# One array for all eight PSUM banks, in a planner-ordered two-layer transformer kernel on one core

## The chip, the core and the metric

The kernel runs on one core of a Trainium2 chip. It is one launch. The metric is the device time of that launch in microseconds: the median of three runs of the kernel before is 1513.48 us (1513.02 to 1515.63). The engines are TensorE (PE, with its weight loads as PEld), VectorE (DVE), ScalarE (ACT), GpSimd (POOL) and SyncE (SP), which issues most transfers.

## The reference

Two transformer layers on x of 2048 rows by 256 columns, all in 32 bits. Each layer adds to x the normed output of an attention block, and then the normed output of a gated FFN. Cut to what matters:

```python
x = x + _layernorm(_L0_attn_ref(_layernorm(x), ...))   # latent q and kv, rotary, 16 heads of 16, causal
x = x + _layernorm(_L0_ffn_ref(_layernorm(x), ...))    # silu(x wg * sg) * (x wu * su), then wdown * sd; int8 weights
x = x + _layernorm(_L1_attn_ref(_layernorm(x), ...))   # plain qkv, 16 heads of 16, causal
x = x + _layernorm(_L1_ffn_ref(_layernorm(x), ...))
# attention: softmax(q k^T * scale + causal mask) v, then the output projection
```

## The kernel before, in words

**Units.** The 2048 rows are cut into four chunks of 512 (CH), and each chunk into four tiles of 128. Sixteen heads are taken in four groups of four (NG). One *unit* is a chunk c of queries with a group g of heads: 16 units a layer, in the order (0,0), (0,1), then all groups of chunks 1, 2 and 3, then (0,2), (0,3) (L780). Each unit has two parts.

**Maxima** (L611 to 697). The largest score of each query row is found first, so that the softmax can subtract it. For each of two head pairs i and each half e of PE's rows, a *fill* (L628 to 631) multiplies a query tile with 512 keys into one PSUM bank named m, and a DVE reduce (L656) takes its row maxima. Fills use 64 of PE's 128 rows: e = 0 the upper half, e = 1 the lower, and the two halves can work side by side. A unit has 8c fills for each pair beside the diagonal ones: `diagonal` (L636) fills two banks with the mask and the scores, `block` b and c fill what lies under the diagonal. `close` (L675) joins the maxima, PE transposes them (mt, L692), and ACT copies them into mrow (L696).

**Weighted sum** (L699 to 763). For each key tile kt and each pair i, PE writes the score pair s: two banks side by side, first minus the maximum (a selector times mrow, L716), then K times Q added to it (L721). ACT takes the exp of both banks in one instruction (L726, 1024 columns), POOL zeroes what lies above the diagonal (L730), and PE adds V times the result into the bank av (L737), which stays in use for the whole unit. At the unit's end ACT copies av out (L745), PE transposes it (ot, L750) and DVE divides (L757, L759).

**Projections and FFN.** `proj0`, `proj1` and `qkv_heads` make Q, K and V of a chunk; Q and K go to DRAM and come back stacked (L460 to 475). `mixed` (L765) is the output projection. `ffn` (L803) runs per chunk eight steps of gate and up (a pair of banks gu, L868), then silu on ACT (L875), the product on DVE (L877), a high part on ACT (L879) and the low rest on POOL (L880), and the down products dn (L835), which add up in two banks over eight steps.

**What sets the order.** The kernel hands every piece of work to a `Plan` (L96) as an operation with an engine, an estimated time, its buffers and a rank (its due time in units). `Plan.run` (L122) sets the order of each engine's queue before the program exists: it repeats a choice of the operation that can start first by its own clock, and among those of that engine within NEAR (0.3 us) of it the one of the lowest rank. An operation can start when those it depends on have ended plus HOP, when its buffers are free plus HOP, and when its engine (on PE: its row half) is free; a change of PE's mode (row halves, column groups, full) adds SWITCH. `lag` is added after an operation's end for those that depend on it. The engines then run their queues in order, and waits are put between them where a buffer is read, written or used again. The fills of unit n have ranks from n - 1.4 on, the scores of unit n from n on, so that the maxima of the next unit stand beside the weighted sum of this one.

**PSUM before.** There are eight banks of 512 columns. They are bound to three pools (L198 to 200): `ps` has two pairs (s and gu), `ps_m` three single banks, all under the tag m (fills, transposes, projections, dn, fz, mt, ot, wo), `ps_av` one bank (av). Each is a ring: its places are given in turn, and the next one may be taken when all that used it have been put in the order.

```python
ps = ctx.enter_context(tc.tile_pool(name="ps", bufs=2, space=PSUM))       # pairs: s, gu
ps_m = ctx.enter_context(tc.tile_pool(name="ps_m", bufs=3, space=PSUM))   # single banks: m
ps_av = ctx.enter_context(tc.tile_pool(name="ps_av", bufs=1, space=PSUM)) # av
```

Of the kernel before, what the change touches and what calls it, by code (L numbers as in the profile page):

```python
# [11 lines left out]
F32 = mybir.dt.float32  # L12
# [51 lines left out]
class Buf:  # L64


    def __init__(self, make, ring=None):
        self.make, self.ring = make, ring
        self.tile = None
        self.users, self.writers, self.readers = [], [], []  # L70
        if ring is not None:
            ring.asked.append(self)
# [15 lines left out]

class Op:
# [6 lines left out]
class Plan:  # L96
# [3 lines left out]
    HOP, NEAR, SWITCH = 0.15, 0.3, 0.25  # L100
# [21 lines left out]
    def run(self):  # L122
# [9 lines left out]
        while ready:  # L132
            best = []
            for o in ready:
                at = max((d.end + self.HOP for d in o.after), default=0.0)
                wanted = {}
                for b in o.bufs:
                    if b.ring is not None and b.tile is None:
                        ring = b.ring
                        n = wanted.get(ring, 0)  # L140
                        wanted[ring] = n + 1
                        if ring.ordered and ring.asked[ring.given + n] is not b:
                            at = None
                            break
                        old = ring.slots[(ring.at + n) % len(ring.slots)]
                        if old is not None:
                            if any(u.end is None for u in old.users):
                                at = None
                                break
                            at = max(at, max(u.end for u in old.users) + self.HOP)  # L150
# [13 lines left out]
            for b in o.bufs:  # L164
                if b.ring is not None and b.tile is None:
                    b.ring.slots[b.ring.at] = b
                    b.ring.at = (b.ring.at + 1) % len(b.ring.slots)
                    b.ring.given += 1
                b.t
# [19 lines left out]
def kernel(ctx: ExitStack, tc: tile.TileContext, x_in, cols_in, rows_in, wd_in, wuq_in, rot_in,  # L189
# [8 lines left out]
    ps = ctx.enter_context(tc.tile_pool(name="ps", bufs=2, space=PSUM))  # L198
    ps_m = ctx.enter_context(tc.tile_pool(name="ps_m", bufs=3, space=PSUM))
    ps_av = ctx.enter_context(tc.tile_pool(name="ps_av", bufs=1, space=PSUM))  # L200


    rings = {}

    def new(pool, shape, dtype, tag, name, n):

        ring = rings.setdefault(tag, Ring(n, tag not in ("m", "s")))
# [3 lines left out]
    def bank(name):  # L211
        return new(ps_m, [P, CH], F32, "m", name, 3)
# [6 lines left out]

    def psum2(name):  # L220
        return ps.tile([P, 2, CH], F32, tag="s", name=name)

    def psum1(name):
        return ps_m.tile([P, CH], F32, tag="m", name=name)
# [375 lines left out]
    def attention(layer, plan, wo, wob, bo, scale):  # L600
        L, KS, Vs, kb, vb = layer.L, layer.K, layer.V, layer.kb, layer.vb
        with tc.tile_pool(name=f"kv{L}", bufs=1) as kv, tc.tile_pool(name=f"at{L}", bufs=1) as at:
# [8 lines left out]
            def maxima(n, c, g, qb):  # L611
# [10 lines left out]
                def block(name, i, e, terms, us, reduces, red_us, kc, dst):  # L622
# [10 lines left out]
                    plan.op("PE", us, fill, r=[qb, kb[kc][g]], w=[s], hold=[dst], rank=rk, mode="row", lanes=(e,), lag=0.3)  # L633
                    plan.op("DVE", red_us, lambda: reduces(s.t), r=[s], w=[dst], rank=rk)

                def diagonal(i):  # L636
# [14 lines left out]
                    plan.op("PE", 1.2, fill, r=[qb, kb[c][g], mask_b, mx_b], w=ss, hold=[pm], rank=rk, mode="row", lag=0.3)  # L651
                    for e in range(2):
                        plan.op("DVE", 0.63, lambda e=e: top(pm.t[:, :, e, i, 1], tiles(ss[e].t)), r=[ss[e]], w=[pm], rank=rank())
# [7 lines left out]
                for i in range(2):  # L661
                    diagonal(i)
                    for e in range(2):
                        block("b", i, e, [(3, 0, 3 * P, 0), (1, 0, P, 3 * P)], 0.4,
                              lambda s, i=i, e=e: top(pml.t[:, e, i, 0:4], tiles(s)), 0.63, c, pml)
# [3 lines left out]
                    for t in range(TPC):  # L669
                        for p in range(c):  # L670
                            for e in range(2):
                                block(f"{t}{p}", i, e, [(t, 0, CH, 0)], 0.22,
                                      lambda s, i=i, e=e, t=t, p=p: top(pm.t[:, t, e, i, 2 + p:3 + p], s), 0.63, p, pm)
# [25 lines left out]
            def weighted(n, c, g, qb, mrow):  # L699
                av = Buf(lambda: ps_av.tile([P, CH], F32, tag="av", name=f"av{L}{n}"), rav)  # L700
# [3 lines left out]
                for kt in range(last + 1):  # L704
# [3 lines left out]
                    for i in range(2):  # L708
                        s = new(ps, [P, 2, CH], F32, "s", f"s{L}{n}{kt}{i}", 2)
# [3 lines left out]
                        def score(s=s, kt=kt, i=i, off=off, nq=nq):  # L713
# [5 lines left out]
                            for e in range(2):  # L719
# [5 lines left out]
                                mode="row", lag=0.3)  # L725
# [52 lines left out]
            rav = Ring(1)  # L778
# [24 lines left out]
    def ffn(L, sg_at, su_at, after=()):  # L803

        with tc.tile_pool(name=f"fw{L}", bufs=1) as fw, tc.tile_pool(name=f"ff{L}", bufs=1) as ff:
# [54 lines left out]
            for n_, c in enumerate(order):  # L860
                halves = []
                for fc in range(8):
                    rk = 10 * n_ + fc
                    s = new(ps, [P, 2, CH], F32, "s", f"gu{L}{c}{fc}", 2)
# [189 lines left out]
```

## Time and profile before

| what | before |
|---|---|
| median of 3 runs | 1513.48 us (1513.02 to 1515.63) |
| the profiled execution's own time | 1515.71 us |
| its span, first to last instruction | 1513.8 us |
| mean granted TensorE clock | 0.934 |
| ACT exp, L726, 640 instructions | 546.3 us busy |
| PE score pair, L716 and L721, 2560 instructions | 331.5 and 298.8 us busy |
| PE av, L737, 2560 instructions | 303.0 us busy |
| HBM read and written | 41.66 and 35.65 MB |

The two attention layers lie at about 60 to 655 us and 800 to 1366 us, the FFNs at 655 to 780 us and from 1366 us to the end. One ot (L750) stands at each unit's end; in the first layer those of chunk 3 are at 502.5, 548.5, 589.7 and 625.0 us.

How to read it: the page gives each engine's busy time, its share of the span, and the costliest groups of instructions with the idle time before them and what ended it. PE's matmuls are pipelined and their ends are modelled, so that PE can be called busy while its next matmul waits. PEld is the load of the weights of a matmul and shows waits that PE itself hides. The waits view sums who waited for whom: total, times, the longest. The windows view gives each engine's busy time in a stretch of the span, the granted clock and the transfers.

### The profile page before, as it was taken

To read this page: it belongs to the slowest core of one execution; us is meant where nothing else is said; L and a number is where in the kernel's file an instruction comes from. 1 tells how busy PE (TensorE), PEld (TensorE's weight loads), DVE (VectorE), ACT (ScalarE), POOL (GpSimd) and SP (SyncE) were. 2 spreads that over 40 slices of the span, in tenths; PEclk is the share of its full clock that TensorE was granted. 3 is DMA by queue.
4 is the path that set the end of the run, shared out by engine and by line. 5 is a ranking of instruction groups with operands and counts; after the bars stand their busy time and mean duration, and the time that the engine had idled before them with its cause. 6 is when DMAs were issued, how large, how long until landed. Compare 5 with 4: busy or idle time off the path is not lost. (4 is left out here: it accounts for less than half of the span.)

```text
span 1513.8 us, 22232 instructions
## 1 busy us (share of the span) xinstructions
PE 1352.8 (89%) x8632; PEld 767.1 (51%) x8632; DVE 936.8 (62%) x1932; ACT 798.5 (53%) x1094; POOL 289.5 (19%) x468
## 2 busy tenths in 40 slices
PE   2468999999999999869878999999999999986986
PEld 2234455555555454436745555555555454444764
DVE  1266578859897883335434668886898888234432
ACT  1232555555556667646443255555655676754553
POOL 2011101110001000235523010110000100033543
PEclk9686999999999999979978699999999999988998
DMA  4532040022000000020045222004000000000000
GB/s 145 183 128 93 27 168 15 15 88 108 15 15 1 15 15 15 1 70 1 1 167 204 72 74 84 15 15 174 22 15 15 15 1 15 15 1 1 15 15 28
DMA packets 42617, 78.74 MB, mean 52 GB/s; under 512 B 3891, under 2 KB 8336, under 8 KB 42384
## 3 DMA queue, kind: packets, MB, share of 16 engines
q1 hardware_dynamic: 42080, 75.85, 14.4%
q8 instruction: 68, 1.11, 0.3%
q0 software_dynamic: 144, 1.16, 0.2%
q10 hardware_dynamic: 288, 0.31, 0.1%
q14 instruction: 37, 0.30, 0.1%
HBM read 41.66 MB, written 35.65 MB: 51 GB/s over the span
## 5 line engine op out<-in xcount | busy, mean ns | idle before, releaser
L726 ACT ACTIVATE pt<-s 128x1024 f32<-128x1024 f32 (+3 forms) x640 | 546.3, 895 | 350.6 <-PE s L721 343.2
L656 DVE TENSOR_REDUCE pm<-m 128x1 f32<-128x512 f32 x768 | 476.2, 682 | 55.3 <-PE m L630 49.9
L716 PE MATMUL s<-mrow,sel 64*128 64x512 f32 (+3 forms) x1280 | 331.5, 405 | 6.9 <-ACT mrow L696 4.6
L737 PE MATMUL av<-pt,V 128*32 128x512 f32 (+3 forms) x2560 | 303.0, 548 | 2.9 <-POOL pt L730 2.9
L721 PE MATMUL s<-Q,K 64*128 64x512 f32 (+3 forms) x1280 | 298.8, 367 | 0.0
L630 PE MATMUL m<-K,Q 64*128 64x512 f32 x768 | 284.7, 489 | 9.1 <-DVE pm L656 0.4
L730 POOL TENSOR_SCALAR_AFFINE_SELECT pt<-pt 128x256 f32<-128x256 f32 x256 | 103.0, 407 | 832.5 <-ACT pt L726 830.5
L716 PEld LDWEIGHTS s<-mrow,sel 64*128 64x128 f32 x1280 | 174.1, 189 | 86.6 <-ACT pt L726 54.4
L630 PEld LDWEIGHTS m<-K,Q 64*128 64x128 f32 x768 | 119.5, 188 | 181.8 <-DVE pm L656 150.5
L721 PEld LDWEIGHTS s<-Q,K 64*128 64x128 f32 x1280 | 188.8, 190 | 11.9
L877 DVE SCALAR_TENSOR_TENSOR fu<-gu,cols,sl 128x512 f32<-128x512 f32 x64 | 47.6, 747 | 88.0 <-ACT sl L875 88.0
L880 POOL TENSOR_TENSOR fl<-fu,fh 128x512 fp32r<-128x512 f32 x64 | 82.1, 1287 | 99.7 <-ACT fh L879 99.7
L737 PEld LDWEIGHTS av<-pt,V 128*32 128x32 f32 x2560 | 52.3, 109 | 87.6 <-issue 72.2
L868 PE MATMUL gu<-fx,wg 128*128 128x512 f32 x256 | 77.2, 424 | 10.5 <-DVE fu L877 4.2
L868 PE MATMUL gu<-fx,wu 128*128 128x512 f32 x256 | 72.5, 407 | 0.0
L875 ACT ACTIVATE sl<-gu,cols 128x512 f32<-128x512 f32 x64 | 43.7, 687 | 39.9 <-PE gu L868 39.6
L868 PEld LDWEIGHTS gu<-fx,wg 128*128 128x128 f32 x256 | 49.3, 201 | 27.6 <-DVE fu L877 9.2
L879 ACT CAST fh<-fu 128x512 fp32r<-128x512 f32 x64 | 39.5, 621 | 36.8 <-DVE fu L877 36.8
L835 PE MATMUL dn<-fh,wdn 128*128 128x512 f32 x128 | 52.9, 413 | 3.6 <-ACT yn_f L402 2.3
L868 PEld LDWEIGHTS gu<-fx,wu 128*128 128x128 f32 x256 | 50.5, 198 | 11.2 <-issue 0.5
L835 PE MATMUL dn<-fl,wdn 128*128 128x512 f32 x128 | 52.3, 409 | 0.3
L428 PE MATMUL tr_f<-ident,xn_f 128*128 128x128 f32 x64 | 16.0, 335 | 28.2 <-ACT xn_f L402 25.5
(763 smaller groups left out, 1449.9 us busy)
## 6 DMA issues: line engine op xcount, KB each, us to landing
K<-sc_k SPq DMA_DIRECT2D x32, 512.0 KB
Q<-sc_q SPq DMA_DIRECT2D x32, 512.0 KB
sc_k<-kh SPq DMA_DIRECT2D x32, 256.0 KB
sc_k<-kl SPq DMA_DIRECT2D x32, 256.0 KB
sc_q<-qh SPq DMA_DIRECT2D x32, 256.0 KB
sc_q<-ql SPq DMA_DIRECT2D x32, 256.0 KB
x<-in_x_dram SPq DMA_DIRECT2D x4, 512.0 KB
out_dram<-x SPq DMA_DIRECT2D x4, 512.0 KB
```

Of the source, the lines that this page charges most:

```text
L630: nc.tensor.matmul(s.t[:, to:to + k1 - k0], qb.t[b:b + 64, i, t * P:(t + 1) * P], KS[kc][b:b + 64, 2 * g + i, k0:k1], start=True, stop=True)
L656: nc.vector.tensor_reduce(dst, src, AX.X, ALU.max)
L716: nc.tensor.matmul(s.t[:, e, 0:nq], sel[b:b + 64, i, :], mrow.t[b:b + 64, off:CH], start=True, stop=False)
L721: nc.tensor.matmul(s.t[:, e, 0:nq], KS[kt // TPC][b:b + 64, 2 * g + i, k * P:(k + 1) * P], qb.t[b:b + 64, i, off:CH], start=False, stop=True)
L726: plan.op("ACT", 0.19 + nq / 620, lambda s=s, pt=pt, nq=nq: nc.scalar.activation(pt.t[:, :, 0:nq], s.t[:, :, 0:nq], AF.Exp, scale=scale), ...
L730: plan.op("POOL", 0.41, lambda pt=pt: nc.gpsimd.affine_select(out=pt.t[:, :, 0:P], in_=pt.t[:, :, 0:P], compare_op=ALU.is_ge, fill=0.0, ba ...
L737: nc.tensor.matmul(av.t[32 * j:32 * j + 32, off:CH], Vs[kt // TPC][:, kt % TPC, DV * h:DV * h + 32], pts[kt, j // 2].t[:, j % 2, 0:nq], st ...
L835: nc.tensor.matmul(dn[dh].t, wdn[:, fc, dh * P:(dh + 1) * P], halves[fc][j].t, start=fc == 0 and j == 0, stop=fc == 7 and j == 1)
L868: nc.tensor.matmul(s.t[:, i, :], w[:, cc, fc * P:(fc + 1) * P], xT[j].t[:, cc, :], start=n == 0, stop=n == 3)
L875: plan.op("ACT", 0.69, lambda s=s, sl=sl, fc=fc: nc.scalar.activation(sl.t, s.t[:, 0, :], AF.Silu, scale=col(sg_at + fc)), r=[s], w=[sl], ...
L877: plan.op("DVE", 0.75, lambda s=s, sl=sl, fu=fu, fc=fc: nc.vector.scalar_tensor_tensor(fu.t, s.t[:, 1, :], col(su_at + fc), sl.t, ALU.mult ...
L880: plan.op("POOL", 1.3, lambda fu=fu, fh=fh, fl=fl: nc.gpsimd.tensor_tensor(fl.t, fu.t, fh.t.bitcast(F32), ALU.subtract), r=[fu, fh], w=[fl ...
```

## The change

All eight PSUM banks become one array of 8 x 512 columns, and the planner gives out its banks. A new class `Banks` keeps who holds each bank. `soonest` says when a single bank, or two neighbouring ones, can be had; `give` takes the bank that is free first (a pair from the low end, a single one from the high end). A pair is given in the order in which pairs were asked for, and only while fewer than two pairs have readers that are not yet in the order; a single bank has no order and no limit. av, which had a bank of its own, is asked for like the rest. Beside that, the planner's constants change: HOP from 0.15 to 0.06, the lag of row-mode operations from 0.3 to 0.2, the estimate of a reduce from 0.63 to 0.60.

```diff
 class Buf:
-    def __init__(self, make, ring=None):
+    def __init__(self, make, ring=None, banks=0):
...
-        if ring is not None:
+        if ring is not None and banks != 1:
             ring.asked.append(self)
...
+class Banks:
+    def __init__(self, n):
+        self.slots, self.asked, self.given, self.limit = [None] * n, [], 0, 2
+    def ready(self, i):
+        users = self.slots[i].users if self.slots[i] else ()
+        return None if any(u.end is None for u in users) else max((u.end for u in users), default=-1.0)
+    def choices(self, k):
+        at = [self.ready(i) for i in range(len(self.slots))]
+        return [(max(at[i:i + k]), i) for i in range(len(at) - k + 1) if None not in at[i:i + k]]
+    def pairs(self):
+        return sum(self.ready(i) is None and self.slots[i].banks == 2 for i in range(len(self.slots))) // 2
+    def soonest(self, b, others):
+        if b.banks == 2 and (self.asked[self.given] is not b or self.pairs() == self.limit):
+            return None
+        free = sorted(t for t, _ in self.choices(b.banks))
+        return free[others] if len(free) > others else None
+    def give(self, b, now):
+        t, i = min((max(t, now), i if b.banks == 2 else -i) for t, i in self.choices(b.banks))
+        b.at = range(abs(i), abs(i) + b.banks)
+        for i in b.at:
+            self.slots[i] = b
+        if b.banks == 2:
+            self.given += 1
...
-    HOP, NEAR, SWITCH = 0.15, 0.3, 0.25
+    HOP, NEAR, SWITCH = 0.06, 0.3, 0.25
...
                     if b.ring is not None and b.tile is None:
                         ring = b.ring
+                        if b.banks:
+                            soonest = ring.soonest(b, banks)
+                            banks += 1
+                            if soonest is None:
+                                at = None
+                                break
+                            at = max(at, soonest + self.HOP)
+                            continue
...
-    ps = ctx.enter_context(tc.tile_pool(name="ps", bufs=2, space=PSUM))
-    ps_m = ctx.enter_context(tc.tile_pool(name="ps_m", bufs=3, space=PSUM))
-    ps_av = ctx.enter_context(tc.tile_pool(name="ps_av", bufs=1, space=PSUM))
+    ps = ctx.enter_context(tc.tile_pool(name="ps", bufs=1, space=PSUM))
...
+    psum, banks = ps.tile([P, 8, CH], F32, tag="banks", name="banks"), Banks(8)
...
     def bank(name):
-        return new(ps_m, [P, CH], F32, "m", name, 3)
+        b = Buf(lambda: psum[:, b.at[0], :], banks, 1)
+        return b
+    def two_banks(name):
+        b = Buf(lambda: psum[:, b.at[0]:b.at[0] + 2, :], banks, 2)
+        return b
...
-                av = Buf(lambda: ps_av.tile([P, CH], F32, tag="av", name=f"av{L}{n}"), rav)
+                av = Buf(lambda: psum[:, av.at[0], :], banks, 1)
...
-                        s = new(ps, [P, 2, CH], F32, "s", f"s{L}{n}{kt}{i}", 2)
+                        s = two_banks(f"s{L}{n}{kt}{i}")
```

The gate and up pairs of the FFN change in the same way as s. In the row-mode operations (fills, diagonals, scores) `lag=0.3` becomes `lag=0.2`, and in the four reduces of 512 columns `0.63` becomes `0.60`.

## The prediction

> **What bounds the kernel now.** I read the page first, for each engine's share and its costliest groups.
>
> ```profile
> span 1513.8 us, 22232 instructions
> ...
> PE 1352.8 (89%) x8632; PEld 767.1 (51%) x8632; DVE 936.8 (62%) x1932; ACT 798.5 (53%) x1094; POOL 289.5 (19%) x468
> ...
> L656 DVE TENSOR_REDUCE pm<-m 128x1 f32<-128x512 f32 x768 | 476.2, 682 | 55.3 <-PE m L630 49.9
> ...
> L630 PE MATMUL m<-K,Q 64*128 64x512 f32 x768 | 284.7, 489 | 9.1 <-DVE pm L656 0.4
> ```
>
> PE looks full and seems never to wait for the reduce (0.4 us). That is an effect of how a matmul's end is drawn: a stalled fill hides under the drawn tail of the matmul before it. So the next view is the waits, where PE's weight loads stand by themselves.
>
> ```profile
> PEld m L630 <- DVE pm L656: 150.5, 309, 0.8
> ...
> PEld s L716 <- ACT pt L726: 54.4, 87, 1.1
> ...
> DVE pm L656 <- PE m L630: 49.9, 104, 2.3
> ```
>
> PE waits for DVE 309 times, and DVE waits for PE 104 times: each starves the other, as a short queue between two engines does. The timeline shows one such stall.
>
> ```profile
> 541.70 0.19 PEld L630 LDWEIGHTS m<-K,Q 64*128 64x128 f32 x2 [0.62 <-DVE pm L656]
> 541.70 1.08 PE L630 MATMUL m<-K,Q 64*128 64x512 f32 x3
> 542.28 0.18 PEld L630 LDWEIGHTS m<-K,Q 64*128 64x128 f32 x1 [0.40 <-DVE pm L656]
> 542.28 0.29 PEld L716 LDWEIGHTS s<-mrow,sel 64*128 64x128 f32 x2
> 542.29 0.72 PE L716 MATMUL s<-mrow,sel 64*128 64x512 f32 x2
> ```
>
> Two fills start at 541.70 on the two row halves of PE; the third needs a bank and starts 0.58 us later, and the score pair behind it waits too. A 512-column matmul holds its half for 0.23 us (start to start in the same timeline), so about 0.35 us is lost. "PE busy" covers all of it.
>
> I then took each matmul's start from the trace and subtracted the earliest one its half allowed (the last start there plus 0.446 ns a column). What is left before fills that wait for DVE is 107 us in the whole run. A single fill that leaves the other half idle before a score pair costs another 58 us. The windows view says in which stages DVE could take more.
>
> ```profile
> 200.00:280.00 80.00, 77.78 (x576) 41.68 (x574) 69.50 (x135) 41.59 (x54) 9.65 (x24) 1.00 0.17 62
> ...
> 410.00:450.00 40.00, 39.19 (x279) 20.23 (x276) 36.26 (x67) 22.07 (x26) 3.25 (x8) 1.00 0.04 14
> 450.00:503.00 53.00, 52.59 (x378) 27.55 (x377) 42.19 (x82) 34.01 (x42) 6.85 (x11) 1.00 0.04 11
> 503.00:549.00 46.00, 45.62 (x346) 22.95 (x344) 37.66 (x69) 29.71 (x35) 3.20 (x8) 1.00 0.04 13
> ```
>
> Columns are length, then PE, PEld, DVE, ACT, POOL busy, granted clock, DMA. In 200 to 280 and 410 to 450 DVE is 87 and 91% busy, so it nearly bounds; from 450 on it is 80% and PE bounds.
>
> **The change, part by part.** All sums are against the profiled execution, 1515.7 us (span 1513.8 and 1.9 around it); the median shown is 1513.5, 2.2 lower.
>
> *A, stages where DVE nearly bounds* (200 to 280, 345 to 450, 920 to 1000, 1055 to 1163: 373 us). DVE is busy 327.3 us there and idle 45.7. PE's stall on fills by the sum above is 51.4. With more banks a fill can be made while more reduces are queued, so both shrink together, and the gain is at most the smaller, 45.7. By how much: in the built order of the changed kernel PE waits for DVE before 482 fills instead of 970 (180 wait for ACT, whose banks they take over), and the DVE instructions still unfinished when a fill may start rise from 3.7 to 4.9 on average. I take half: 23 us. Bounds 0 and 45.7.
>
> A rule speaks against this part. The Trainium skill's first page, Trainium Kernel Development and Optimization, section Best Practices, says to mind PSUM pressure because tiling TensorE speeds the matmuls and not the emptying of PSUM. Here the reduce that empties a bank still takes 0.60 us from start to start, so by the rule A is worth nothing and the sum below is 23 us smaller. The row says that DVE still has 12% idle in these stages, two thirds of its idle time between 130 and 590 (64.7 of 99 us) being before a reduce. I follow the row, but only by half.
>
> *B, stages where PE bounds* (450 to 590, 1163 to 1303: 280 us). Stall on fills 13.0 us, halves left idle by single fills 17.5. In the built order, runs of fills of odd length go from 336 to 166, about half, and the waits halve as well: 15 us. Bounds 0 and 30. The depth rises least here (3.4 to 3.8).
>
> *C, stages with a chunk's projection inside* (130 to 200, 280 to 345, 873 to 920, 1000 to 1055). Stall 20.8, half: 10 us. Bounds 0 and 20.8.
>
> *Entries and the rest.* From 780 to 873 PE stalls 16.2 us on fills, but a straight run of 38 fills is limited by the reduces themselves; nothing. Before 130 PE waits for loads (23.9 us for the rotation, 16.7 and 9.4 for K and Q); nothing. The FFNs keep gate-and-up in pairs and get one more single bank. At the end, dn at 1491.23 waited 1.81 us for yn_f to free a bank, then ran 8.2 us; in the new order three of its eight steps stand ahead of the last gate-and-up. For both FFNs and the attention tails I take 3 us; bounds -3 and 8.
>
> *What is added.* The single array makes ACT and DVE wait for each other's earlier read of the same bank. By their place those waits are over already: PE's write between them waited for the first read. The cost is the extra wait instruction: DVE 132 to 270, ACT 752 to 791, PE 110 to 58. Their durations in the trace are 21, 17 and 51 ns: 2.9 + 0.7 - 2.7, about 1; with those on DVE in its saturated stages I take 2. The score fills get a new wait: 270 of them now wait for a reduce, none to speak of before. Behind such a fill stands everything in PE's queue, and the exp on ACT waits for it, then the select on POOL and av. Before, fills that waited for DVE lost 107 us over 970 waits, 0.11 each: 270 of those are 30 us. The nearest row is the score pair's own wait for ACT, where almost no start was late beyond what its half allowed: 0. I take 8; bounds 0 and 30.
>
> *Planner constants and moved steps.* HOP goes from 0.15 to 0.06, the row lag from 0.3 to 0.2, the reduce from 0.63 to 0.60. The trace gives 0.053 from a reduce's end to the weight load, 0.598 from reduce to reduce, and 0.527 from a fill's start to its reduce when DVE is idle; old terms gave 0.67 for that, new ones 0.48. They are closer in all three, a little early in the last. No gain is taken for this alone; it is part of the new order. On SP all 226 transfers remain and 15 stand elsewhere: four loads of Q later, two earlier, one kept q and two loads of K by some places. Q and K loads landed ahead of need in all attention stages but the entry; nothing, up to 3 if one is late. Mode changes of PE go from 761 to 768: nothing.
>
> Sum: 23 + 15 + 10 + 3 - 2 - 8 = 41 us. 1515.7 - 41 = 1474.7, and by the median 1472.5: 1473.
>
> A second rule would bear on B: TensorE: Matmul & The Clock Gate, section A second HAM failure mode, reports that cycling through PSUM banks left PE idle for moments so often that its clock went back and forth between half and full. The rows have 1.00 in every stage from 345 to 590, with three banks cycled and a stall in nearly each tile, so I charge nothing; by the rule, half of B's 280 us at half clock would lose 70.
>
> **Rivals.**
> *DVE stays the bound (0.20).* Then A is nothing: 41 - 23 = 18, so 1495. For it: 91% in 410 to 450. Against: the mutual waits.
> *The queue pays in full (0.12).* A 45.7, B 30, C 20.8, 3, -2: 97, so 1416; with a third of it lost to placement, 1440. For it: the waits on both sides. Against: the depth in B hardly grows.
> *Score pairs starve (0.15): slower.* A pair needs two free neighbouring banks and single fills may take any. If each of the 270 new waits costs more than 0.18 us the gain of 49 is gone; at 0.25 (half a stalled third fill, with ACT idle behind it) they cost 68, so 1513.5 + 19 = 1532. For it: fills have lower ranks than the scores of the unit before and go first. Against: the new order still has two score pairs in nearly every tile of av.
> *It does nothing (0.06).* The order hardly matters because PE's sum of work is the same: 1513.
>
> **How the numbers follow.** My forecast has 0.47: 1473. Faster by more than 0.2% (3 us, about what a measurement here can tell from no change): 0.47 + 0.20 + 0.12 = 0.79. Within: 0.06. Slower: 0.15. The range goes from 1438, which leaves part of the full-pay case out, to 1516, which leaves most of the starved case out.
>
> **What would show it.** Right: PE's weight loads wait for DVE at most half of 150 us; DVE is over 92% busy in the stages of A; a unit of the last chunk takes 43 us instead of 46 (from one ot to the next, near 503 to 549). The starved case would show as PE's score loads waiting for DVE for tens of us and ACT's wait for scores above 343. The DVE-bound case would leave the stages of A as long as they are. I am wrong if PE's gain in A is eaten by the in-order queue: a fill put early because HOP is short, and the pair behind it late.

## The result, and the profile after

The changed kernel takes 1490.3 us in the median of four runs (1488.0 to 1492.2), against 1514.6 us for the kernel before on the same chip: a ratio of 0.984 (0.982 to 0.986), 24 us less. The forecast was 1473: the sign and the range held, the gain was 24 instead of 41. The profiled execution's own time is 1490.08 us, its span 1488.4. One execution of the last kernel told of below, the kernel before with shorter reduces, ran at a mean granted clock of 0.666 and took 1736 us; it is left out, and all others have 0.924 to 0.946.

The page after, busy time first, then the reduce and the fill:

```profile
span 1488.4 us, 22354 instructions
...
PE 1325.1 (89%) x8632; PEld 740.4 (50%) x8632; DVE 934.5 (63%) x1932; ACT 798.0 (54%) x1094; POOL 289.6 (19%) x468
...
L701 DVE TENSOR_REDUCE pm<-banks 128x1 f32<-128x512 f32 (+1 forms) x896 | 557.8, 682 | 144.0 <-PE banks L675 73.4
...
L675 PE MATMUL banks<-K,Q 64*128 64x512 f32 (+3 forms) x1152 | 261.8, 414 | 16.7 <-ACT pt L771 3.5
```

All tiles in PSUM are now called banks, so rows join that were apart; lines moved too (the fill from L630 to L675, the reduce from L656 to L701, the selector of the score pair from L716 to L761, the exp from L726 to L771). The reduce still costs 682 ns. PE is called busy for 28 us less with the same 8632 matmuls: that is stall under drawn tails, not work.

The waits view after. Each row gives total us, times, and the longest:

```profile
ACT pt L771 <- PE banks L766: 332.6, 328, 9.2
PEld banks L761 <- ACT pt L771: 99.2, 138, 1.2
...
DVE pm L701 <- PE banks L675: 73.4, 105, 2.0
...
PEld banks L675 <- DVE pm L701: 62.1, 146, 1.1
PEld banks L761 <- DVE pm L701: 56.9, 85, 1.4
...
PE banks L693 <- DMA Q<-sc_q: 32.1, 3, 12.1
...
PEld banks L675 <- ACT pt L771: 24.4, 54, 0.9
```

Fills (L675) waiting for the reduce fell from 150.5 to 62.1 us. But score pairs (L761) now wait 56.9 us for reduces, which they did not before; fills wait 24.4 us for exps; and score pairs wait 99.2 us for exps instead of 54.4. The rows of before and after are not quite alike: before, the smaller fill blocks had tile names of their own and stood in rows apart. Summed by source line, fills waited 194.1 us for reduces before and wait 82.3 now, score pairs 0 and 63.4. With the waits for exps, all of it was 194.1 + 54.4 = 249 us before and is 82.3 + 63.4 + 24.4 + 99.2 = 269 us now. Such sums are not time on the path (PE's two halves wait at once, and a wait can lie under the matmul before it), but they warn that the waits moved rather than went.

**Where the time went.** I cut both traces at the ot transposes that end the units. Chunk 1 of layer 0 here reaches from the start of the kernel, that of layer 1 from the end of layer 0's attention, so that it holds the first FFN. "Last" are the two units of chunk 0 at the end of a layer. Lengths in us:

| stretch | before | after | array, old constants | constants, old pools | HOP 0.14 | bank times forgotten |
|---|---|---|---|---|---|---|
| start and chunk 1 | 279.4 | 264.5 | 266.1 | 277.1 | 279.0 | 265.2 |
| chunk 2 | 170.6 | 173.6 | 167.8 | 173.0 | 183.4 | 169.2 |
| chunk 3 | 175.0 | 177.5 | 175.5 | 180.1 | 174.4 | 175.5 |
| last | 28.9 | 26.9 | 26.4 | 27.9 | 25.8 | 25.3 |
| FFN, layer 1 to chunk 1 | 344.7 | 339.0 | 341.3 | 342.5 | 343.0 | 358.3 |
| chunk 2 | 164.3 | 167.7 | 162.1 | 168.6 | 164.4 | 162.1 |
| chunk 3 | 174.9 | 177.6 | 175.5 | 180.4 | 173.6 | 175.5 |
| last | 27.1 | 23.8 | 23.0 | 25.4 | 23.0 | 23.0 |
| second FFN | 149.0 | 137.8 | 138.3 | 143.1 | 137.3 | 143.5 |
| span | 1513.8 | 1488.4 | 1475.9 | 1518.3 | 1503.9 | 1497.6 |

(The last four columns are experiments told below. All lengths are of one profiled execution each; that of HOP 0.14 was 6 us slower than the median of its kernel.) Chunks 2 and 3, where the forecast saw most of the gain, are *longer* after, by 3.0 + 2.5 + 3.4 + 2.7 = 11.6 us. The start (14.9), the second FFN (11.2), the stretch with the first FFN (5.7) and the ends of the layers (5.3) are shorter.

Such a cut moves work as well as time: chunk 2 of each layer holds 99 exps after instead of 93, and the stretch before it 80 instead of 87. Some of what chunk 2 is longer by was shifted into it. Over a whole layer up to the end of chunk 3 the work is the same in every trace (308 exps, 630 reduces). There layer 0 is 9.4 us shorter after (625.0 to 615.6), and layer 1 with the first FFN is no shorter (683.8 and 684.3). So the gain is 9.4 in layer 0, 5.4 in the ends of attention and 11.2 in the second FFN.

A unit of chunk 3, the one told of in the prediction, went from 46.0 to 47.1 us. The windows view shows it; columns are length, then PE, PEld, DVE, ACT, POOL busy, granted clock, DMA. Before:

```profile
502.50:548.50 46.00, 45.62 (x345) 22.95 (x344) 37.66 (x69) 29.71 (x35) 3.20 (x8) 1.00 0.04 13
```

After:

```profile
489.50:536.60 47.10, 44.68 (x340) 21.25 (x336) 36.55 (x67) 28.38 (x33) 3.21 (x8) 1.00 0.04 13
```

DVE did not fill up: 78% busy in the unit after, 82% before.

### The profile page after: what moved, and what is told of

It is laid out like the page before. It is cut to its first block, busy times and chain, and to the rows that moved or that the text cites. A ratio compares the mean times of both kernels' runs of the same rounds, so it can differ in the third digit from the quotient of the medians.

```text
span 1488.4 us, 22354 instructions
## 1 busy us (share of the span) xinstructions
PE 1325.1 (89%) x8632; PEld 740.4 (50%) x8632; DVE 934.5 (63%) x1932; ACT 798.0 (54%) x1094; POOL 289.6 (19%) x468
## 4 chain that ended last, share of the span: by engine, by line
PE 64%; DVE 18%; ACT 6%; DMA 4%; POOL 3%; issue 3%; SPq 1%; POOLq 0%; ACTq 0%; DVEq 0%
PE banks L782 13%; PE banks L761 11%; DVE pm L701 11%; PE banks L675 9%; PE banks L766 8%; PE banks L553 8%; PE banks L912 5%; ACT pt L771 3%; PE banks L693 2%; DVE pml L701 2%; PE banks L688 2%; PE banks L879 2%; DMA Q<-sc_q 2%; PE banks L473 2%; PE banks L795 1%
## 5 line engine op out<-in xcount | busy, mean ns | idle before, releaser
L771 ACT ACTIVATE pt<-banks 128x1024 f32<-128x1024 f32 (+3 forms) x640 | 548.1, 895 | 362.2 <-PE banks L766 332.6
L701 DVE TENSOR_REDUCE pm<-banks 128x1 f32<-128x512 f32 (+1 forms) x896 | 557.8, 682 | 144.0 <-PE banks L675 73.4
L782 PE MATMUL banks<-pt,V 128*32 128x512 f32 (+3 forms) x2560 | 303.5, 545 | 6.7 <-POOL pt L775 6.4
L761 PE MATMUL banks<-mrow,sel 64*128 64x512 f32 (+3 forms) x1280 | 296.3, 429 | 14.6 <-DVE pm L701 5.2
L675 PE MATMUL banks<-K,Q 64*128 64x512 f32 (+3 forms) x1152 | 261.8, 414 | 16.7 <-ACT pt L771 3.5
L766 PE MATMUL banks<-Q,K 64*128 64x512 f32 (+3 forms) x1280 | 257.8, 373 | 0.0
L761 PEld LDWEIGHTS banks<-mrow,sel 64*128 64x128 f32 x1280 | 139.7, 191 | 197.1 <-ACT pt L771 99.2
L675 PEld LDWEIGHTS banks<-K,Q 64*128 64x128 f32 x1152 | 138.3, 192 | 142.7 <-DVE pm L701 62.1
L701 DVE TENSOR_REDUCE pml<-banks 128x4 f32<-128x512 f32 (+1 forms) x256 | 129.7, 549 | 95.1 <-PE banks L675 94.7
L766 PEld LDWEIGHTS banks<-Q,K 64*128 64x128 f32 x1280 | 143.6, 193 | 7.1
L693 PE MATMUL banks<-K,Q 64*128 64x128 f32 x512 | 46.9, 307 | 32.1 <-DMA Q<-sc_q 32.1
L693 PEld LDWEIGHTS banks<-K,Q 64*128 64x128 f32 x512 | 37.5, 207 | 62.6 <-issue 49.8
L919 ACT ACTIVATE sl<-banks,cols 128x512 f32<-128x512 f32 x64 | 43.1, 687 | 15.2 <-PE banks L912 14.9
```

The lines of the kernel that those rows point to most:

```text
L675: nc.tensor.matmul(s.t[:, to:to + k1 - k0], qb.t[b:b + 64, i, t * P:(t + 1) * P], KS[kc][b:b + 64, 2 * g + i, k0:k1], start=True, stop=True)
L693: nc.tensor.matmul(ss[e].t[:, at_], qb.t[b:b + 64, i, at_], KS[c][b:b + 64, 2 * g + i, at_], start=False, stop=t == TPC - 1)
L701: nc.vector.tensor_reduce(dst, src, AX.X, ALU.max)
L761: nc.tensor.matmul(s.t[:, e, 0:nq], sel[b:b + 64, i, :], mrow.t[b:b + 64, off:CH], start=True, stop=False)
L766: nc.tensor.matmul(s.t[:, e, 0:nq], KS[kt // TPC][b:b + 64, 2 * g + i, k * P:(k + 1) * P], qb.t[b:b + 64, i, off:CH], start=False, stop=True)
L771: plan.op("ACT", 0.19 + nq / 620, lambda s=s, pt=pt, nq=nq: nc.scalar.activation(pt.t[:, :, 0:nq], s.t[:, :, 0:nq], AF.Exp, scale=scale), ...
```

## Experiments

My theory after the result had two parts: the array lets PE and DVE wait less for each other, but where PE bounds, that wait is replaced by another; and the new constants, taken at nothing, cost time. The rivals were that the constants are the gain and the banks do nothing, and that DVE is the bound everywhere. All kernels below were timed against the kernel before on the same chip; medians of the kernel before lay between 1512.8 and 1514.6. With shared banks "the array" is all eight in one; "bound" means fixed places for scores, single tiles and av.

**The two halves of the change.** First the constants alone, in the kernel before:

```diff
-    HOP, NEAR, SWITCH = 0.15, 0.3, 0.25
+    HOP, NEAR, SWITCH = 0.06, 0.3, 0.25
...
-                    plan.op("PE", us, fill, r=[qb, kb[kc][g]], w=[s], hold=[dst], rank=rk, mode="row", lanes=(e,), lag=0.3)
+                    plan.op("PE", us, fill, r=[qb, kb[kc][g]], w=[s], hold=[dst], rank=rk, mode="row", lanes=(e,), lag=0.2)
...
-                                      lambda s, i=i, e=e, t=t, p=p: top(pm.t[:, t, e, i, 2 + p:3 + p], s), 0.63, p, pm)
+                                      lambda s, i=i, e=e, t=t, p=p: top(pm.t[:, t, e, i, 2 + p:3 + p], s), 0.60, p, pm)
...
```

The other row-mode operations and reduces of 512 columns change alike (three places in the text for each of the two).

> The kernel before with the planner's new constants alone (HOP 0.06, row lag 0.2, reduce 0.60) and the three old pools. If the array is what gains, 1510 to 1517. If the order from the better constants is what gains, about 1490 to 1500. If the short constants cost time in the in-order queues (theory: they are why the middle attention stages of the changed kernel got 4 to 6 us longer), over 1518.

Measured: 1518.4 us, ratio 1.0034 (1.0022 to 1.0046), 5 us slower.

Then the array alone, that is, the changed kernel with these lines turned back:

> The changed kernel with the old constants (HOP 0.15, row lag 0.3, reduce 0.63): the array alone. If the array is what gains and the constants add nothing, 1485 to 1495. If the short constants cost time in the middle attention stages, less than 1485. If the gain needs both, 1500 to 1515.

Measured: 1478.0 us, ratio 0.978 (0.974 to 0.982): 35 us faster than before, and 12 us faster than the change as made. So the gain comes with the banks, and in these orders the constants add a loss: 5 us with the old pools, 12 with the array. (How much of such a loss is chance is asked below.) In the table the constants lengthen every chunk 2 and 3 (by 2 to 6 us with either set of banks). They shorten the second FFN by 5.9 with the old pools and do nothing there with the array.

The array alone moves the waits in the same way, a little less strongly:

```profile
PEld banks L761 <- ACT pt L771: 102.4, 151, 1.6
...
PEld banks L675 <- DVE pm L701: 78.2, 174, 1.1
...
PEld banks L761 <- DVE pm L701: 39.2, 64, 1.7
```

Even so, its chunks 2 and 3 are only 170.6 + 175.0 + 164.3 + 174.9 - (167.8 + 175.5 + 162.1 + 175.5) = 3.9 us shorter than before. (Here too two exps more lie in each chunk 2. Over a whole layer to the end of chunk 3, layer 0 is 15.5 us shorter and layer 1 4.9.)

**Which part of the kernel needs the array.** In the changed kernel, the attention plans got fixed banks again (pairs at 0 and 2, singles 4 to 6, av 7), the FFN kept the array:

```diff
-        return [(max(at[i:i + k]), i) for i in range(len(at) - k + 1) if None not in at[i:i + k]]
+        own = self.zones[kind] if self.zones else range(len(at) - k + 1)
+        return [(max(at[i:i + k]), i) for i in own if None not in at[i:i + k]]
...
+            banks.zones = {"pair": (0, 2), "one": (4, 5, 6), "av": (7,)}
...
+            banks.zones = None
```

The first assignment stands ahead of each attention plan's run, the second ahead of each FFN plan's.

> The changed kernel, but in both attention plans the banks are bound as before (two pairs, three single banks, one for av); shared only in the FFN plans. If the gain is the FFNs' (each stage 11 us shorter in the changed kernel), about 1490 or less. If attention's sharing carries it, as the prediction's parts A, B and C had it, 1505 or more.

Measured: 1517.6 us, ratio 1.0032 (1.0021 to 1.0043). With its constants it is to be held against the constants alone (1518.4): sharing in the FFN is worth 0.7 us by the medians, 5.3 in the second FFN by the profiled executions (137.8 against 143.1). And against the change as made, sharing in attention is worth 27.3 us. The fixed places of this run are given by which is free first, where the pools before gave them in turn; by its time that rule is worth nothing of its own.

The other way round, attention shared and the FFN bound, with the two assignments exchanged:

```diff
+            banks.zones = None
...
+            banks.zones = {"pair": (0, 2), "one": (4, 5, 6), "av": (7,)}
```

> The changed kernel, shared in both attention plans and bound as before (two pairs, three single banks) in the FFN plans. The other half: if the gain is the FFNs', 1508 to 1520; if attention's sharing carries it, 1490 to 1495.

Measured: 1522.2 us, ratio 1.0053 (1.0038 to 1.0067). The two halves do not add up to the whole: against the constants alone they give -0.7 and +3.8 us where the whole gives -28.1. The traces say where. In layer 1's chunks 2 and 3 this kernel is as long as the changed one, at the start and in layer 0 within 4 us. But the stretch with the first FFN and layer 1's chunk 1 takes 366.2 us instead of 339.0, and 17.8 of these 27 lie between the ot at the end of unit 0 and that of unit 2 (79.7 against 61.9). This is the first sign of something the prediction had not considered, taken up under "a new deal of the order" below.

Sharing without exchange: the array with the old constants, but in attention pairs keep banks 0 to 3 for themselves, and single tiles and av share 4 to 7:

```diff
+            banks.zones = {"pair": (0, 2), "one": (4, 5, 6, 7), "av": (4, 5, 6, 7)}
```

> The array with the old constants, but in the attention plans score pairs have banks 0 to 3 for themselves and single fills and av share 4 to 7, so that no score pair waits for a reduce. If score pairs waiting for fills' banks hold the array back, less than 1475. If it's the free exchange of banks between pairs and singles that gains, 1485 to 1505. If neither, 1478.

Measured: 1502.5 us, ratio 0.995 (0.992 to 0.997). Of the array's 35 us, 25 go when scores and fills can't take each other's banks. By this pair of runs it is the exchange and not av's bank alone; the runs below show that as much as 22 of the 25 could be luck of the order.

**Which constant costs the 12 us.** One at a time, from the changed kernel: HOP back to 0.15, then instead the row lag back to 0.3.

```diff
-    HOP, NEAR, SWITCH = 0.06, 0.3, 0.25
+    HOP, NEAR, SWITCH = 0.15, 0.3, 0.25
```

> The changed kernel with HOP alone back at 0.15; the row lag stays 0.2 and the reduce 0.60. If the short HOP is what cost about 12 us beside the array-alone kernel, 1476 to 1481. If the shorter lag and reduce are, about 1490.

Measured: 1491.1 us, ratio 0.985 (0.983 to 0.987).

```diff
-                    plan.op("PE", us, fill, r=[qb, kb[kc][g]], w=[s], hold=[dst], rank=rk, mode="row", lanes=(e,), lag=0.2)
+                    plan.op("PE", us, fill, r=[qb, kb[kc][g]], w=[s], hold=[dst], rank=rk, mode="row", lanes=(e,), lag=0.3)
```

> The changed kernel with the row lag alone back at 0.3; HOP stays 0.06 and the reduce 0.60. If the lag (reduce and exp expected 0.1 us too early after their fills) is what cost, 1476 to 1481; if HOP is, about 1490. If both halves of the slack do the same thing, both this and the HOP run lie between, 1480 to 1486.

Measured: 1495.6 us, ratio 0.989 (0.986 to 0.991). Neither brings the 12 us back; the second loses 5 more. That left the reduce's estimate, tried from the other side, on the array with the old constants:

```diff
-                                      lambda s, i=i, e=e, t=t, p=p: top(pm.t[:, t, e, i, 2 + p:3 + p], s), 0.63, p, pm)
+                                      lambda s, i=i, e=e, t=t, p=p: top(pm.t[:, t, e, i, 2 + p:3 + p], s), 0.60, p, pm)
```

> The array with the old constants (1478), but with the estimate of a reduce at 0.60 in place of 0.63 and nothing else. Going back in HOP alone or in the lag alone left the time of the changed kernel within 6 us of where it was, so the third constant is left. If the reduce estimate is what costs the 12 us: 1487 to 1494. If each small change of a constant only deals a new order, good or bad by chance: anywhere from 1475 to 1500, with no one constant to blame. If two constants have to change together: 1478.

Measured: 1481.7 us, ratio 0.979 (0.976 to 0.982), whose interval overlaps that of 0.63 (0.974 to 0.982). So in these runs no single constant carries the 12 us.

**A new deal of the order.** Then a change that can mean nothing for the chip, on the array with the old constants:

```diff
-    HOP, NEAR, SWITCH = 0.15, 0.3, 0.25
+    HOP, NEAR, SWITCH = 0.14, 0.3, 0.25
```

> The array with the old constants, but HOP 0.14 in place of 0.15: a change too small to mean anything about the chip, which still gives another order on every engine. If the time follows what the constants say: 1478, within 3 us. If the order is an accident of small differences, the time moves by 5 us or more in either direction, and the 12 us between the array alone and the changed kernel are of that size.

Measured: 1499.5 us, ratio 0.990 (0.988 to 0.992). A hundredth of a microsecond in an estimate costs 21.5 us. The planner takes the operation that can start first by its own clock, so a small shift swaps two operations, and everything after them falls differently. In the table the loss is at the start and in chunk 2 of layer 0 (+12.9, +15.6), and chunk 3 is faster by 1 to 2 us.

And one more of that kind: the bank times that the planner carries over from the plan before are forgotten before each plan.

```diff
+            banks.slots = [None] * 8
```

> The array with the old constants; before each of the three plans that are made (two attention stages with an FFN behind them) the planner forgets when its banks came free in the plan before, whose clock is not the new plan's. Where the leftover times hold back the first pieces of a stage in the order, the stretch from the end of layer 0's attention through layer 1's first units becomes shorter: 5 to 15 us, so 1463 to 1473. If they only shift everything by the same amount: 1478, within 5.

Measured: 1500.0 us, ratio 0.991 (0.990 to 0.993): 22 us slower instead of faster, my expectation had the wrong sign. Chunks 2 and 3 stay as they were, but for 1.4 us; the stretch with layer 1's entry grows by 17.0 and the second FFN by 5.2. The leftover times, which mean nothing, had helped.

The windows view shows what such a bad stretch is. In this kernel, at the entry of layer 1:

```profile
848.00:872.00 24.00, 23.89 (x64) 13.63 (x64) 22.73 (x41) 1.17 (x2) 0.00 (x0) 0.50 0.00 1
872.00:878.00 6.00, 5.64 (x21) 3.14 (x23) 3.42 (x11) 0.00 (x0) 0.00 (x0) 0.50 0.00 0
```

The same place with the array as it was:

```profile
844.00:856.00 12.00, 10.97 (x54) 5.27 (x54) 11.90 (x27) 0.59 (x1) 0.21 (x1) 0.83 0.01 1
856.00:862.00 6.00, 6.00 (x33) 3.79 (x34) 4.16 (x8) 2.02 (x5) 0.77 (x2) 0.78 0.13 42
```

For 24 us DVE does one reduce after another (95% busy), ACT hardly anything, and PE's granted clock is at half. Fills stand in a row in PE's queue with no score pair between them (42 fills from 846 to 866 us), and PE gives them out no faster than DVE reduces them; the exps and av products that could run beside them come later. With the array as it was, this lasts half as long. I counted such time in each trace (the middles of all stretches of 4 us in which DVE is over 93% and ACT under 12% busy): 14 us in the array alone, 32 us with the bank times forgotten (+18, and the span +21.7), 40 us with HOP 0.14 (+26, and the span +28.0), 30 us with the FFN bound (16 in the changed kernel). For the first two it is about as much as the whole loss, which makes it a likely cause (no run changed it alone). It does not explain the changed kernel (16) or that with the lag turned back (18), which are 12 and 21 us longer in span than the array alone.

The clock is a rival. In the traces the granted clock is 1.00 or 0.50, and the time at 0.50 is 176 us in the array alone, 198 with the bank times forgotten, 223 with HOP 0.14, 196 in the changed kernel and 214 with the lag turned back: every slower deal has more of it. The executions of one kernel share one order and still differ in it: in the four kernels with 14 or more executions in one round, the span grows by 0.26 to 0.35 us for each us more at half clock (taken as twice the span's share that the mean clock lacks). At about 0.3, the means of all executions (176 us in the array alone; 196, 210, 194 and 200 in the other four, in the same order) make 5 to 10 us. That is an estimate, of a quarter to a half of the losses, and whether the clock is the cause there or only a sign of an idle PE was not tested. It does not rank all kernels: the constants in the old pools have 178 us at half clock and 1518.4 us.

**What the reduce costs.** The last pair asks DVE directly. Row maxima of whole earlier blocks (768 reduces) take only the first 256 of the 512 columns; the maxima of the other half are left out. The order on every engine stays the same. On the array with the old constants:

```diff
-                                      lambda s, i=i, e=e, t=t, p=p: top(pm.t[:, t, e, i, 2 + p:3 + p], s), 0.63, p, pm)
+                                      lambda s, i=i, e=e, t=t, p=p: top(pm.t[:, t, e, i, 2 + p:3 + p], s[:, 0:CH // 2]), 0.63, p, pm)
```

> The array with the old constants and the same order on every engine, but the reduces of the 512-column blocks of earlier chunks take only the first 256 columns (the row maximum of the other half is left out; fills are whole). Each such reduce gets about 0.27 us shorter, 768 of them. If DVE bounds the middle stages, those of chunk 2's maxima (108 to 111 us each) shrink by 10 us or more, and the run ends near 1440 to 1455. If the in-order PE queue bounds (its waits for exp and its mode changes), they shrink by under 4 us and the run ends at 1468 or more.

Measured: 1449.2 us, ratio 0.957 (0.955 to 0.960), 28.8 us below the array alone. The same edit in the kernel before:

> The kernel before, in its own order on every engine, with the 768 row maxima of whole earlier blocks taken over the first 256 of their 512 columns only; the maxima of the other half of the columns are left out. The same edit took 29 us from the array with the old constants (to 1449). If the array gains by hiding the reduces, the kernel before must have more to gain from shorter ones: 29 + about 36 = 60 to 65 us, so about 1450. If the array gains by something else (other places in the order, the FFN, the entries), the edit takes about 29 us here too: about 1484.

Measured: 1463.2 us, ratio 0.967 (0.965 to 0.968), 50.2 us below the kernel before. (No trace of this kernel is used.) In both the edit shortens the same reduces; in the traced pair, with the array, their busy time falls from 476 to 282 us. In the kernel before that is worth 50 us, with the array 29. So in these two orders the array hides about 21 us of what the reduces cost, and leaves 29. The expectation had 60 to 65 for the kernel before if the array gained by hiding alone, and 29 if it did not hide at all: it lies between, and about 35 - 21 = 14 of the array's 35 us are something else (the second FFN is 10.7 shorter). Each half of this comparison keeps its order, but the two orders differ, and another deal could move the 21 as it moves the time.

The windows view of the array alone in the last three units of chunk 2 and in chunk 3 of layer 0:

```profile
323.00:433.90 110.90, 108.16 (x813) 52.49 (x811) 95.94 (x180) 66.13 (x78) 9.80 (x24) 1.00 0.16 55
433.90:609.40 175.50, 173.99 (x1343) 84.84 (x1343) 111.53 (x215) 123.08 (x145) 17.76 (x38) 1.00 0.03 10
```

and with the half reduces:

```profile
316.30:423.10 106.80, 103.07 (x813) 50.68 (x811) 66.14 (x178) 65.68 (x78) 9.76 (x24) 1.00 0.16 57
423.10:597.30 174.20, 172.51 (x1346) 83.30 (x1344) 80.75 (x214) 123.25 (x145) 17.68 (x38) 1.00 0.03 10
```

In chunk 3 DVE has 31 us less to do and the stretch is 1.3 us shorter: DVE holds hardly anything up there. In the three units of chunk 2 DVE has 30 us less to do and 4.1 are gained. By the parts of the prediction, the half reduces gain 14.1 us in the stages of A, 11.8 in those of C (8.8 of it at layer 1's entry, where the fills come in rows) and 2.7 in those of B.

## Why the prediction was right in sign and wrong in size

By the prediction's own parts, cut at the unit ends nearest to its limits, the change in length is, in us:

| part | forecast | after | array, old constants |
|---|---|---|---|
| A | -23 | +5.0 | -0.9 |
| B | -15 | +5.2 | +1.2 |
| C | -10 | -4.4 | 0.0 |
| entry of layer 0, to the end of unit 0 | 0 | +1.6 | -4.0 |
| first FFN and layer 1's unit 0 | in the 3 below | -16.4 | -16.7 |
| ends of attention | in the 3 below | -5.4 | -6.7 |
| second FFN | -3 | -11.2 | -10.8 |

The forecast charged 10 us more for added waits. The -16.4 is matched by the stage of C behind it, from 873 to 919 us before, which is 15.4 longer: 15 reduces moved into it over the unit's end. That is work shifted, not gained. So the three parts that were to bring 48 us brought none (5.8 longer), and most of the gain stands where 3 was forecast. That the sum came out within the range is luck.

*The waits (first mark).* "PE's weight loads wait for DVE at most half of 150 us": 62.1, right for the fills (by source line 82.3 of 194.1). As a mark for time it was wrong, because the score pairs took over 56.9 of it.

*A, 23 us: failed.* The step was "both shrink together, and the gain is at most the smaller", of which I took half. A's stages are 5.0 us longer after, with 59 matmuls more in them (2758 instead of 2699), and 0.9 shorter with the array alone, with 56 more. For the same work that is about nothing. Nor is it likely that a deeper queue could have brought 23 by freeing DVE: the half reduces, in the array's order, free it far more and gain 14.1 here. I redid the prediction's own sum (each matmul's start less the earliest that its half allowed) for the last three units of layer 0's chunk 2. It is an estimate, since the trace does not name the half. Fills that waited for DVE had 15.6 us before and have 5.9 after. But fills that wait for ACT went from 0.4 to 3.8, score pairs that wait for ACT from -2.5 to 1.6 (the earliest start is an estimate, so it can be below nothing), score pairs that wait for DVE from 0 to 2.0, and changes of PE's mode behind a wait for ACT from 1.4 to 4.2. The total is 41.1 before and 41.2 after. (The stretch itself is 5.7 us longer; 73 exps with their matmuls lie in it instead of 65.) The timeline after shows one such exchange:

```profile
410.00 0.40 PE L766 MATMUL banks<-Q,K 64*128 64x512 f32 x2
410.26 0.29 PEld L675 LDWEIGHTS banks<-K,Q 64*128 64x128 f32 x3 [0.30 <-DVE pm L701]
410.26 1.24 PE L675 MATMUL banks<-K,Q 64*128 64x512 f32 x5
410.80 3.08 DVE L701 TENSOR_REDUCE pm<-banks 128x1 f32<-128x512 f32 x5 [0.59 <-PE banks L675]
411.00 0.19 PEld L675 LDWEIGHTS banks<-K,Q 64*128 64x128 f32 x2 [0.44 <-ACT pt L771]
```

The fill at 410.26 had waited 0.30 us for a reduce, and then DVE has nothing queued and idles 0.59: no fill had been made ahead. At 411.00 a fill waits 0.44 us for a bank that an exp must empty; in the pools before, no fill had an exp to wait for. PE's queue is in order and there are still eight banks: a place that a fill borrows is missing for the next score pair. This is the prediction's own sign of being wrong, "PE's gain in A is eaten by the in-order queue", but not for the reason given there, a short HOP: with the old HOP and lag score pairs wait 39.2 us for reduces all the same. The mark "DVE is over 92% busy in the stages of A" failed as well (84.7 to 86.3%).

*B, 15 us: failed.* The step was that half of the fills' stall and of the idle halves goes and the time goes with it. Chunk 3 of both layers is 5.2 us longer after, and 1.2 longer with the array alone, and the unit that was to take 43 us takes 47.1. The half reduces, which take away much of the reason to wait for DVE, gain 1.3 us per layer here. In all the traces used, chunk 3 takes 173.6 to 180.6 us. So DVE does not bound it, and PE's own order of work is what is left; what in PE's queue sets the 174 us (mode changes, single fills) wasn't tried.

*C, 10 us, and entries, nothing: the place was right in layer 0 only.* There the first stage of C (130 to 201 us) is 16.1 us shorter after, and the start and chunk 1 together 14.9. But that gain depends on the order: with HOP 0.14 it is 0.4, with the lag turned back 3.3 (276.1). In layer 1 the first FFN, the entry and C together gain 1.9. There PE waits 12.1 us for one load of Q, where it waited 3.9 before (all three such waits: 29.7 us before, 32.1 after) and where the prediction took loads at "nothing, up to 3".

*FFNs and tails, 3 us: too small.* 11.2 in the second FFN and 5.3 in the two ends of attention. The step named was right (three of the eight down products ahead of the last gate-and-up, and no down product waits for yn_f any more). The array alone gains 10.8 here, the constants alone in the old pools 5.9; the two do not add up.

*Score pairs' new wait, 8 us: right that it exists.* 56.9 us over 85 waits, 0.67 us each, longer than the 0.11 it was sized by. Its share of the time can't be told apart from A's loss: the two are one exchange. ACT's wait for scores did not rise above 343 (332.6), so the starved case as priced did not come. The added wait instructions, taken at 2 us, can't be sized either: 21 and 17 ns are their medians, after as before, but DVE's 270 lasted 247 ns on the mean and ACT's 791 206 ns, as some now hold idle time themselves.

*Constants, nothing: not borne out.* In these orders they cost 12 us with the array and 5 without. Comparing each constant with the nearest measured gap said that they were closer to the chip; that did not make the order better. As a shift that means nothing costs more than 12, the 12 can't be laid to their values.

*The rules weighed.* Mind PSUM pressure (the Trainium skill, Trainium Kernel Development and Optimization, Best Practices), by which A was worth nothing, came nearer than my half: the array alone gives 0.9 us in A's stages, where shorter emptying gives 14.1 more. In B the clock stayed at 1.00 before and after, so charging nothing for the clock was right there.

*The rivals.* DVE as the bound had named 1495, close to 1490. Its sign came true, the stages of A stayed about as long as they were, but it would have given B its 15 and C its 10. In the case that pays in full, a third of 97 lost gives about 1449, not 1440. That the order hardly matters was the least true: it moves the time by 22 us.

Summed: A, B and C got 5.8 us longer where 48 shorter was forecast, 54 too little gain; the other stretches gained 31.4 where 3 was forecast, 28 more; and the 10 charged for added waits are in these. 54 - 28 - 10 is the 16 that the span misses. The array alone at 1478 comes close to the forecast of 1473, and not for its reasons.

**What stays open.** Seven kernels with the array in attention and in the FFN, which differ in planner constants or leftovers only, lie at 1478, 1482, 1490, 1491, 1496, 1499.5 and 1500 us; three with bound attention at 1513.5, 1517.6 and 1518.4. The array is faster in every one of them. So the gain is the array's, but its size, 13 to 35 us, is in good part the order's. The 12 us between the change and its better version, and the 25 of pairs in banks of their own, are hardly larger than the 22 us that a meaningless shift moves; their cause beyond "another order" isn't settled. The kernel with the FFN alone bound (1522) is slower than the kernel before although attention shares its banks; 27 of the 32 us by which it is longer than the changed kernel lie in the stretch with layer 1's entry. How much of these losses is the clock's is open too.

## What to carry to other kernels

A stall that the trace puts on one engine is worth removing only where nothing else then holds PE up: check with a run that makes the suspected engine's work shorter in the same order (here 50 us before, 29 after, 1.3 in a chunk 3 for which 7.5 was forecast) before banks are rearranged for it. When a greedy planner sets the order, time a few meaningless perturbations of its constants before a difference of one or two per cent is put down to a design, and keep the best order: here the array with the old constants, 1478 us. Look for stretches where one engine runs alone, such as rows of fills without scores, which went with the loss in two of the bad orders. And count work as well as time when stretches of two orders are compared.

## What the runs showed of the hardware

The granted clock was 0.50 for 24 us in the row of fills shown above, whose pace DVE sets and in which PE is called over 99% busy. It isn't so in every such row: in the 12 us shown of the array alone it was 0.83. The Trainium skill (TensorE: Matmul & The Clock Gate, A second HAM failure mode) describes a clock that goes back and forth between half and full where banks are cycled. The prediction set this aside by the rows from 345 to 590, and there the clock stays at 1.00 after the change too. At the entry it was at half for the whole window, so that this is the same thing isn't shown.

What half clock costs a row of matmuls shows in the kernel before. The windows view has a clock of 0.50 from 1491.40 to 1494.70 us and of 1.00 from 1495.00 to 1499.50; the timeline of PE has

```profile
1492.14 0.63 PE L835 MATMUL dn<-fh,wdn 128*128 128x512 f32 x1
1492.57 0.63 PE L835 MATMUL dn<-fl,wdn 128*128 128x512 f32 x1
...
1495.21 0.39 PE L835 MATMUL dn<-fh,wdn 128*128 128x512 f32 x1
1495.43 0.39 PE L835 MATMUL dn<-fl,wdn 128*128 128x512 f32 x1
```

From start to start it is 0.43 us at half clock and 0.22 at full. While DVE sets the pace with a reduce each 0.60 us, this need not cost anything; 6 us later in the window of fills DVE is only 57% busy and the clock is still at half, so some microseconds are probably lost there.

A reduce of half the columns takes 418 ns instead of 682: it is not half.
